# Seven-product matmuls in orders with more products between two uses of a bank

## The chip, the cores and the metric

The kernel runs on one core of a Trainium2 chip. A core has a matrix engine (TensorE, PE in the profile, with its weight loads shown apart as PEld), a vector engine (VectorE, DVE), a scalar engine (ScalarE, ACT), a general engine (GpSimd, POOL) and a synchronization engine (SyncE, SP), which here issues nearly all DMA transfers. Each engine runs its own instructions in order; semaphores make one wait for another. Matmul results go to PSUM, [...]from which ACT and DVE read them.

The metric is the device time of one execution, in microseconds, as the median of several runs. Lower is better.

## The reference

There are 16 independent batch items of 1024 nodes and 256 channels, and one 1024 x 1024 weighted adjacency matrix that they share. All is fp32. Cut to what matters, for each item:

```
# layer 0: attention whose queries come from a weighted graph product
A   = 2*| |sigmoid(diff of node means) - 0.5| - 0.5 |     # symmetrized
g   = relu((x^T @ (adj * A)) * para)                      # queries
k,v = x @ kv_w                                            # keys and values, 4 heads of 64
x   = layernorm(x + softmax(g k^T * scale) v)             # this is x1
# layer 1: two graph convolutions
h   = relu(x @ w1_loop + adj @ (x @ w1_neigh) + b1)       # 256 -> 128
h   = relu(h @ w2_loop + adj @ (h @ w2_neigh) + b2)       # 128 -> 256
x   = layernorm(x + (x + h) / 2)
```

## The kernel before

Items go through a software pipeline, one round per item. In round b the kernel computes the attention of item b, the first graph convolution of item b-1 together with the second of item b-2, the last normalization of item b-3, and the queries, keys and values of item b+1. The loop over b is written out by hand at line 1434; every engine gets its instructions in the order in which the Python code calls them, and nothing is reordered afterwards. Rounds 2 to 14 take the branch at line 1611 for the keys, values and queries, and rounds 2 to 15 compute the inner products below.

Most matrix products are made in the manner of Strassen and Winograd: a product of two-by-two blocks needs seven products instead of eight, of sums of blocks. The code numbers them 1 to 7. The seven are summed in pairs and chains: a PSUM bank gets product 1, is copied to SBUF, then product 6 is added onto it (the argument again=True), it is copied again, and so on. [...]each product that adds onto a bank waits until the copy of that bank has ended. Weights of a product are loaded by an instruction of their own (LDWEIGHTS), which carries the wait.

Three stages of a round concern us.

**Keys and values** (class KeysValues, line 420). Each key product is one call of key (two fp32 matmul records of 512 columns); each value product one call of value (four calls and eight records of 128 columns). start makes products 1 and 2 of both; middle makes 6, 5, 7 and 3, and end makes 4. Keys and values alternate. Products 1, 6, 5 and 3 use the bank k_first (v_first for values), 7 and 4 use k_next (v_next). Copies of banks are on ACT, final additions on DVE. The factors are sums of blocks: those of x are made by DVE (sums, line 430), those of the weights were made once, lie in DRAM as kv_sums and are fetched by load (line 448) in each round: 512 KB on SP's queue, right behind the two 512 KB transfers of para, which the scaling of the queries (line 693) reads. That scaling and the scaling of the normalization are called through later, between the sixth pair of products and the additions.

**Inner products** (fast_inner, line 961). x1 @ w1_neigh and x1 @ w1_loop are one seven-product scheme: with x1's channel-by-node blocks w11, w12, w21 and w22 and sums of them made by DVE in inner_sums (line 949). There are three banks, upper, lower and chain. Product 1 and then 6, 5 and 3 go to chain, 2 to upper, 7 and 4 to lower. The result t1T is transposed and stored to DRAM, to be fetched again by nodes; the other result, loops, holds x1 @ w1_loop until the convolution is done. fast_inner comes after the first half of the attention (both_units, line 785, called with pair 0) and is followed by the scores of the second half. both_units calls part_sum (a row sum for the softmax denominators) and then summed, which is inner_sums.

**The end of the graph convolutions** (Joined.run, line 1304, and last_products, line 1110). The convolution's seven products share their banks with the last products of item b-2. At the end DVE has these steps in order: the sum of u3, settle(1, 1) with it (line 1105: relu, then added to the residual), the addition of the loop terms, loop + first (line 1368), which frees the bank first, then rest, with the products 4 and 3 and their settle steps. The next products on PE, g_ps for the queries, begin in the bank first.

```
            rest = c2.last_products(third, second)
            self.product(3, first, again=True, steps=range(TJ // 2, TJ))
...
                loop = c1.loops[:, FB:N]
                nc.vector.tensor_add(loop, loop, first)
                c1.relu(1, loop)
            rest()
```

Of the kernel before, what the change touches and what calls it, by code (L numbers as in the profile page):

```python
# [18 lines left out]
def kernel(  # L19
# [31 lines left out]
    nc = tc.nc  # L51

    B, N, C = x.shape
# [6 lines left out]
    FB = 512  # L60
# [27 lines left out]
    def half_psum(name):  # L88
        return big_psum(name)[:, 0:FB]

    def bank_psum(name):
        return psum.tile([P, FB], F32, tag="bank", name=name, bufs=2)
# [327 lines left out]
    class KeysValues:  # L420
# [40 lines left out]
        def value(self, n, dst, again=False):  # L461
            for t in range(TJ):
                nc.tensor.matmul(dst[:, ts(t, P)], self.w[n][:, ts(t, P)], self.a[1][n],  # L463
                                 start=not again and t == 0, stop=True, skip_group_check=again or t > 0)

        def run(self, between=lambda: None, later=lambda: None, lowered=lambda: None):
            self.start()
            self.middle(between, later, lowered=lowered)
            return self.end()
# [23 lines left out]
        def block(self, i, j):  # L493
            return self.v[:, ts(j, TJ), ts(i, P)]

        def tiles(self, t):
            return t.rearrange("p (t c) -> p t c", c=P)
# [200 lines left out]
    class Attention:  # L698
# [86 lines left out]
        def both_units(self, pair, first=lambda: None, second=lambda: None, third=lambda: None, summed=None):  # L785
            u = NJ * pair
            self.scores(u, 0)
            self.scores(u + 1, NT, summed=False)
            row = row_tile(f"o_{self.b}_{pair}")
            self.collect(u + 1, 1)  # L790
            first()
            self.collect(u + 1, 2, 3)
            second()
            self.outputs(u, half_psum, turned=False)
            self.collect(u + 1, 4, 5)
            pav, self.o[u] = self.o[u], row
            nc.vector.transpose(row[:, 0:FB], pav)
            self.collect(u + 1, 6, 7)
            accB = self.turned_sum(u + 1)
            if summed:  # L800
                self.part_sum(u + 1, accB)
                summed()
            self.outputs(u + 1, turned=False)
            nc.vector.transpose(row[:, FB:N], self.o.pop(u + 1))
            if not summed:
                self.part_sum(u + 1, accB)
            third()
# [115 lines left out]
    class GraphConv:  # L923
# [25 lines left out]
        def inner_sums(self):  # L949
            w11, w12, w21, w22 = (self.xT[:, cc, ts(j, FB)] for cc in range(NC) for j in range(NJ))  # L950
            t13, t24 = (row_tile(f"X_{self.b}_{k}") for k in range(2))
            t1, t3, t2, t4 = t13[:, 0:FB], t13[:, FB:N], t24[:, 0:FB], t24[:, FB:N]
            nc.vector.tensor_sub(t1, w12, w11)
            nc.vector.tensor_sub(t2, w22, t1)
            nc.vector.tensor_sub(t3, w22, w12)
            nc.vector.tensor_sub(t4, w21, t2)
            s1, s2, s3, s4 = (self.w1[:, ts(n, P)] for n in range(4))
            self.inner_factors = {1: (w1n_sb[:, 0, :], w11), 2: (w1n_sb[:, 1, :], w21), 3: (s4, w22),
                                  4: (w1l_sb[:, 1, :], t4), 5: (s1, t1), 6: (s2, t2), 7: (s3, t3)}

        def fast_inner(self, aside=lambda: None):
            b = self.b

            def product(n, dst, again=False):
                w, xs = self.inner_factors[n]
                nc.tensor.matmul(dst, w, xs, start=not again, stop=True, skip_group_check=again)  # L966

            upper, lower, chain = (half_psum(f"in_ps_{b}_{i}") for i in range(3))
            s12, s34, t1T, self.loops, t1B = (row_tile(f"in_{b}_{i}") for i in range(5))
            p1, u2, u3, p7 = s12[:, 0:FB], s12[:, FB:N], s34[:, 0:FB], s34[:, FB:N]  # L970
            product(1, chain)
            nc.scalar.copy(p1, chain)
            product(2, upper)
            nc.vector.tensor_add(t1T[:, 0:FB], p1, upper)
            aside()
            product(6, chain, again=True)
            nc.scalar.copy(u2, chain)
            product(7, lower)
            nc.scalar.copy(p7, lower)
            product(5, chain, again=True)  # L980
            nc.scalar.copy(u3, chain)
            nc.vector.tensor_add(self.loops[:, FB:N], u3, p7)
            product(4, lower, again=True)
            nc.vector.tensor_add(self.loops[:, 0:FB], u2, lower)
            product(3, chain, again=True)
            nc.scalar.copy(t1T[:, FB:N], chain)
            nc.vector.transpose(t1B, t1T)
            self.t1d = dram.tile([N, HID], F32, tag="t1d", name=f"t1d_{b}", bufs=2)
            for a in range(Q):
                nc.sync.dma_start(out=self.t1d[:, a * S:(a + 1) * S].rearrange("(bn k) r -> k bn r", k=S),  # L990
                                  in_=by_node(t1B[a * S:(a + 1) * S, :]))
# [118 lines left out]
        def last_products(self, a, c):  # L1110
            name = f"h2_{self.b}"
            d = bank_psum(f"{name}_ps")
            snaps = [row_tile(f"{name}_{k}") for k in range(2)]
            p1, u2, u3 = snaps[0][:, 0:FB], snaps[0][:, FB:N], snaps[1][:, 0:FB]
            self.seventh_part(1, a)
            nc.scalar.copy(p1, a)
            self.seventh_part(2, d, start=True)
            nc.vector.tensor_add(p1, p1, d)
            self.settle(0, 0, p1)
            self.seventh_part(6, a)  # L1120
            nc.scalar.copy(u2, a)
            self.seventh_part(5, c)
            self.seventh_part(7, a)
            nc.scalar.copy(u3, a)
            nc.vector.tensor_add(u3, u3, c)
            self.settle(1, 1, u3)

            def rest():
                self.seventh_part(4, a)
                self.settle(1, 0, a)  # L1130
                self.seventh_part(3, c)
                nc.vector.tensor_add(u2, u2, c)
                self.settle(0, 1, u2)

            return rest
# [238 lines left out]
    def run():  # L1374
# [11 lines left out]
        q = Queries(0, x_first)  # L1386
        for t in range(NT):
            q.load(t)
        kv = KeysValues(0, xT)
# [5 lines left out]
        tiles = {mt: adj_blocked(mt) for mt in (0, TJ, 1)}  # L1395
# [34 lines left out]
        kT, v = kv.end()  # L1430
# [3 lines left out]
        for b in range(B):  # L1434
# [8 lines left out]
            if more:  # L1443
                q = (FastQueries if c1 else Queries)(b + 1, xb)
# [63 lines left out]
            elif more:  # L1508
# [10 lines left out]
                def summed():  # L1519
                    c1.inner_sums()  # L1520
                    if c3:
                        c3.deviation_aside()
# [88 lines left out]
            elif both and more:  # L1611
                q.pair(2)
                q.step(0)
                q.step(1, norm.mean, 5)
                q.pair(3)
                norm.squares()
                q.step(2)
                norm.sum_squares()
                q.load_para()
                kv.load()  # L1620
                q.step(3, lambda: norm.variance(bank_psum), 4)
                qT = q.end(kv.sums, lambda: None)
                xB = load_blocked(b + 1, f"a{b + 1}")
                load_next()
                kT, v = kv.run(later=lambda: (q.scale(), norm.scale()))
                norm.spread()
                att.watch()
            elif more:
                q.pair(2)
                q.step(0)  # L1630
                q.step(1, lambda: att.add(3), 5)
                q.pair(3)
                q.step(2, norm.mean)
                q.load_para()
                kv.load()
                q.step(3)
                qT = q.end(norm.sum_squares, norm.squares)
                xB = load_blocked(b + 1, f"a{b + 1}")
                load_next()
                first, second, third = adj_sum_steps(quarters, 3)  # L1640
                kT, v = kv.run(lambda: (first(), norm.variance()), q.scale, second)
                att.watch()
                third()
                norm.scale()
                norm.spread()
            else:
                c2.load_x()
                both.fetch("00", "10", 2, 3)
                c1.load_t1()
                both.left(nc.gpsimd)  # L1650
                both.fetch(1, 4, "11")
                both.run({1: (lambda: att.add_pairs(1), att.watch), 6: (norm.mean, norm.squares, norm.sum_squares),
                          5: (lambda: norm.variance(bank_psum),), 4: (norm.scale, norm.spread)}, last=nc.vector)
                c1.turn(0)
                c1.turn(1)
# [35 lines left out]
    with tc.If(count < P):  # L1691
        with tc.For_i(0, B, 1) as b:
            xb = load_x(b, "z")
            xT = channel_major(load_blocked(b, "z"), "xT_z")
            q = Queries("z", xb)
# [50 lines left out]
```

## Time and profile before

| What | Value |
|---|---|
| Time, median of 3 runs | 2123.66 us (2123.23 to 2124.41) |
| The profiled execution, its own time | 2123.94 us |
| Its span, first to last instruction | 2122.2 us, mean granted TensorE clock 0.999 |
| PE busy | 2106.6 us (99%), 8360 matmul records |
| DVE busy | 1884.2 us (89%) |
| ACT busy | 1251.8 us (59%) |
| POOL busy | 363.6 us (17%) |
| Inner products' matmuls (line 966) | 196 records in 14 stages |
| Key products (line 459) | 224 records |
| Value products (line 463) | 896 records |
| DMA queue of SP | 363.07 MB, 66.5% of the time of 16 engines |

How to read it: a line such as "943.13 1.98 PE L966 MATMUL in_ps<-x1T,w1n_sb 128*128 128x512 f32 x4" of the timeline gives the start, the duration of the merged instructions, the engine, the line of the kernel, the operation, what is written from what, the shapes and how many instructions are merged. In square brackets stand the idle time of the engine before it and what ended it. A row of the table of windows gives a stretch of time, its length, the busy time of each engine in it with the number of its instructions, the granted clock, the mean busy share of a DMA engine and the GB/s moved. Matmuls are pipelined, and the recorded end of one lies beyond the start of the next.

### The profile page before, as it was taken

The numbers are of one execution on the slowest core, as the hardware profiler recorded it, in microseconds if no ns is written. First come the engines' busy times: TensorE is split into PE (matmuls) and PEld (weight loads), VectorE is DVE, ScalarE is ACT, GpSimd is POOL, SyncE is SP. The second block draws the span as 40 slices with busy tenths as digits, with TensorE's granted clock in tenths as the row PEclk, the third lists the DMA queues.
The fourth block names the chain that finished last, engine by engine and source line by source line (L and its number), as shares of the span: only waits on it lengthen the run. The fifth ranks groups of instructions, "written<-read, shape, count | busy, mean of one in ns | idle before, by whom it ended". The sixth has DMA issues, their size and how long they took to land.

```text
span 2122.2 us, 24759 instructions
## 1 busy us (share of the span) xinstructions
PE 2106.6 (99%) x8360; PEld 996.1 (47%) x8360; DVE 1884.2 (89%) x2212; ACT 1251.8 (59%) x2126; POOL 363.6 (17%) x224
## 2 busy tenths in 40 slices
PE   9999999999999999999999999999999999999998
PEld 5344434445354453544535445354443534445355
DVE  6899998989989899898998989989899898989875
ACT  5845574556756566564765747557475584655523
POOL 2011103131021311213122031210312103131022
PEclk9999999999999999999999999999999999999999
DMA  8495756666648776476764768657596574966455
GB/s 216 122 175 186 150 149 199 124 224 138 185 154 156 244 127 195 151 146 237 139 204 149 139 226 164 208 131 158 195 174 215 134 161 173 184 214 130 140 187 179
DMA packets 688694, 364.98 MB, mean 172 GB/s; under 512 B 550705, under 2 KB 629937, under 8 KB 688561
## 3 DMA queue, kind: packets, MB, share of 16 engines
q1 hardware_dynamic: 688288, 363.07, 66.5%
q8 instruction: 68, 1.11, 0.2%
q14 instruction: 66, 0.53, 0.1%
q10 hardware_dynamic: 272, 0.26, 0.0%
HBM read 305.46 MB, written 57.80 MB: 171 GB/s over the span
## 4 chain that ended last, share of the span: by engine, by line
PE 94%; DVE 3%; DMA 2%; issue 0%; SPq 0%; ACT 0%; POOL 0%; POOLq 0%; DVEq 0%
PE s L726 21%; PE av L772 20%; PE hu_ps L1301 16%; PE g_ps L671 15%; PE v_ps L463 4%; PE k_ps L459 4%; PE in_ps L966 4%; PE hu_ps L1103 4%; PE g_ps L590 2%; DMA kv_sums<-kv_sums 2%; DVE acc L747 1%; PE h_ps L1014 1%; PE u_ps L1043 1%; PE h_ps L1103 1%; PE t_ps L940 0%
## 5 line engine op out<-in xcount | busy, mean ns | idle before, releaser
L747 DVE TENSOR_TENSOR acc<-acc,pr 128x1024 f32<-128x1024 f32 x384 | 481.1, 1253 | 34.3 <-ACT pr L731 0.9
L726 PE MATMUL s<-qT,kT 64*128 64x512 f32 x2048 | 448.9, 593 | 0.0
L772 PE MATMUL av<-pr,v 128*64 128x512 f32 x2048 | 447.0, 594 | 0.0
L733 ACT ACTIVATE pr<-s 128x1024 f32<-128x1024 f32 x392 | 390.9, 1116 | 41.3 <-PE s L726 41.2
L726 PEld LDWEIGHTS s<-qT,kT 64*128 64x128 f32 x2048 | 195.3, 187 | 241.3 <-issue 176.9
L772 PEld LDWEIGHTS av<-pr,v 128*64 128x64 f32 x2048 | 144.0, 137 | 297.3 <-issue 267.4
L1301 PE MATMUL hu_ps<-adj,R 128*128 128x512 f32 x480 | 213.6, 592 | 0.0
L376 POOL TENSOR_TENSOR rstd<-rstd,neg_half 128x32 f32<-128x32 f32 x16 | 88.4, 5522 | 566.7 <-DVE rstd L374 566.7
L582 DVE SCALAR_TENSOR_TENSOR wg<-wg,adj 128x1024 f32<-128x1024 f32 x128 | 168.9, 1358 | 3.6 <-ACT wg L577 3.6
L731 ACT ACTIVATE pr<-s 128x512 f32<-128x512 f32 x240 | 142.4, 702 | 0.0
L576 ACT ACTIVATE wg<-c_row,c_sums 128x1024 f32<-128x1024 f32 x120 | 139.4, 1162 | 2.7 <-DVE accB L754 1.0
L1301 PEld LDWEIGHTS hu_ps<-adj,R 128*128 128x128 f32 x480 | 90.0, 190 | 107.1 <-issue 98.8
L577 ACT ACTIVATE wg<-wg 128x1024 f32<-128x1024 f32 x128 | 135.4, 1057 | 4.1
L1301 PE MATMUL hu_ps<-adj,t 128*128 128x512 f32 x240 | 109.2, 598 | 0.0
L671 PE MATMUL g_ps<-wg,x 128*128 128x512 f32 x224 | 109.0, 599 | 0.0
L671 PE MATMUL g_ps<-T,xB 128*128 128x512 f32 x208 | 107.3, 597 | 0.0
L671 PE MATMUL g_ps<-wg,xB 128*128 128x512 f32 x208 | 106.2, 592 | 0.0
L1324 ACT COPY snap<-hu_ps 128x512 f32<-128x512 f32 x15 | 8.8, 586 | 157.5 <-PE hu_ps L1301 136.2
L1164 POOL TENSOR_TENSOR rstd<-rstd,neg_half 128x8 f32<-128x8 f32 x12 | 19.6, 1637 | 476.4 <-DVE rstd L1163 476.4
L745 DVE TENSOR_TENSOR acc<-pr,pr 128x1024 f32<-128x1024 f32 x64 | 77.9, 1217 | 21.5 <-ACT pr L733 21.5
L1292 POOL TENSOR_TENSOR R<-h 128x512 f32<-128x512 f32 x14 | 20.7, 1476 | 422.5 <-PE av L772 397.2
L754 DVE STREAM_TRANSPOSE accB<-acc 128x1024 f32<-128x1024 f32 x64 | 79.7, 1245 | 3.1
(289 smaller groups left out, 3297.7 us busy)
## 6 DMA issues: line engine op xcount, KB each, us to landing
adj<-adjT SPq DMA_DIRECT2D x210, 512.0 KB
adj<-in_adj_dram SPq DMA_DIRECT2D x128, 512.0 KB
para<-in_L_gnn_para_dram SPq DMA_DIRECT2D x32, 512.0 KB
xB_a<-in_x_dram SPq DMA_DIRECT2D x128, 128.0 KB
x1d<-xB_a SPq DMA_DIRECT2D x128, 128.0 KB
x<-x1d SPq DMA_DIRECT2D x16, 1024.0 KB
xB<-in_x_dram SPq DMA_DIRECT2D x120, 128.0 KB
x<-in_x_dram SPq DMA_DIRECT2D x15, 1024.0 KB
```

What stands on the lines that cost most here:

```text
L376: nc.gpsimd.tensor_tensor(self.rstd, self.rstd, neg_half, ALU.pow)
L576: nc.scalar.activation(wg, self.c_row, AF.Abs, bias=self.c_col[:, t:t + 1], scale=-1.0)
L577: nc.scalar.activation(wg, wg, AF.Tanh, scale=-0.5 / C)
L582: nc.vector.scalar_tensor_tensor(wg, wg, 1.0, self.adj.pop(t), op0=ALU.add, op1=ALU.mult)
L671: nc.tensor.matmul(self.p[n], x_n[:, k, :], w_n, start=(k == 0), stop=(k == TJ - 1))
L726: nc.tensor.matmul(halves[s], self.kT[rows, pair, ts(mt, P)], self.qT[rows, pair, ts(j, FB)], start=True, stop=True)
L731: nc.scalar.activation(pr[:, ts(s, FB)], halves[s], AF.Exp)
L733: nc.scalar.activation(pr, ps, AF.Exp)
L747: nc.vector.tensor_add(self.acc, self.acc, prs[mt])
L772: nc.tensor.matmul(pav[s * HD:(s + 1) * HD, :], self.v[:, mt, pair * P + s * HD:pair * P + (s + 1) * HD], prs[mt][:, ts(s, FB)], start=(mt ...
L1103: nc.tensor.matmul(dst[:, ts(t, P)], a[:, ts(t, P)], w, start=first, stop=True, skip_group_check=not first)
L1301: nc.tensor.matmul(dst, self.x[n][:, k, :], of_rows(rows, k), start=(start and k == 0), stop=(k == TJ - 1), skip_group_check=again)
```

## The change

There are five edits.

- run_spread is new, and takes the place of middle and end in rounds 2 to 14 only. The order of the products becomes 1, 2, 6, 7, 5, 4, 3, keys and values still alternating; later is called after the products 5. Banks and sums stay, so that three products stand between any two on one bank.
- kv.load is called ahead of q.load_para, which puts the transfer of kv_sums ahead of the two of para on SP's queue.
- fast_inner makes 1, 2, 7, 6, 3, 4, 5. Product 3 starts afresh in the bank upper instead of being added onto chain; t1T and loops now get chain by two additions on DVE, where before an ACT copy gave t1T and a DVE addition of two copies gave loops. There is one copy less on ACT and one addition more on DVE in each of the 14 stages.
- inner_sums comes ahead of part_sum in both_units, and makes t3 first.
- settle(1, 1, u3) is moved into rest, behind the addition of the loop terms.

```diff
--- before.py
+++ after.py
@@ -462,6 +462,37 @@
             for t in range(TJ):
                 nc.tensor.matmul(dst[:, ts(t, P)], self.w[n][:, ts(t, P)], self.a[1][n],
                                  start=not again and t == 0, stop=True, skip_group_check=again or t > 0)
+
+        def run_spread(self, later):
+            copy, add = nc.scalar.copy, nc.vector.tensor_add
+            kT, block, tiles = self.kT, self.block, self.tiles
+            (_, u1, u3, p7), (_, z1, z3, y7) = self.ksnap, self.vsnap
+            k_first, v_first = self.k_first, self.v_first
+            self.key(6, k_first, again=True)
+            copy(u1, k_first)
+            self.value(6, v_first, again=True)
+            copy(z1, v_first)
+            k_next, v_next = half_psum(f"k_ps_{self.b}_2"), bank_psum(f"v_ps_{self.b}_2")
+            self.key(7, k_next)
+            copy(p7, k_next)
+            self.value(7, v_next)
+            copy(y7, v_next)
+            self.key(5, k_first, again=True)
+            copy(u3, k_first)
+            self.value(5, v_first, again=True)
+            copy(z3, v_first)
+            later()
+            self.key(4, k_next, again=True)
+            add(kT[:, 1, FB:N], u3, p7)
+            add(kT[:, 1, 0:FB], u1, k_next)
+            self.value(4, v_next, again=True)
+            add(block(1, 1), tiles(z3), tiles(y7))
+            add(block(1, 0), tiles(z1), tiles(v_next))
+            self.key(3, k_first, again=True)
+            copy(kT[:, 0, FB:N], k_first)
+            self.value(3, v_first, again=True)
+            copy(block(0, 1), tiles(v_first))
+            return kT, self.v
 
         def run(self, between=lambda: None, later=lambda: None, lowered=lambda: None):
             self.start()
@@ -798,8 +829,8 @@
             self.collect(u + 1, 6, 7)
             accB = self.turned_sum(u + 1)
             if summed:
+                summed()
                 self.part_sum(u + 1, accB)
-                summed()
             self.outputs(u + 1, turned=False)
             nc.vector.transpose(row[:, FB:N], self.o.pop(u + 1))
             if not summed:
@@ -950,9 +981,9 @@
             w11, w12, w21, w22 = (self.xT[:, cc, ts(j, FB)] for cc in range(NC) for j in range(NJ))
             t13, t24 = (row_tile(f"X_{self.b}_{k}") for k in range(2))
             t1, t3, t2, t4 = t13[:, 0:FB], t13[:, FB:N], t24[:, 0:FB], t24[:, FB:N]
+            nc.vector.tensor_sub(t3, w22, w12)
             nc.vector.tensor_sub(t1, w12, w11)
             nc.vector.tensor_sub(t2, w22, t1)
-            nc.vector.tensor_sub(t3, w22, w12)
             nc.vector.tensor_sub(t4, w21, t2)
             s1, s2, s3, s4 = (self.w1[:, ts(n, P)] for n in range(4))
             self.inner_factors = {1: (w1n_sb[:, 0, :], w11), 2: (w1n_sb[:, 1, :], w21), 3: (s4, w22),
@@ -967,23 +998,23 @@
 
             upper, lower, chain = (half_psum(f"in_ps_{b}_{i}") for i in range(3))
             s12, s34, t1T, self.loops, t1B = (row_tile(f"in_{b}_{i}") for i in range(5))
-            p1, u2, u3, p7 = s12[:, 0:FB], s12[:, FB:N], s34[:, 0:FB], s34[:, FB:N]
+            p1, u2, p3, p7 = s12[:, 0:FB], s12[:, FB:N], s34[:, 0:FB], s34[:, FB:N]
             product(1, chain)
             nc.scalar.copy(p1, chain)
             product(2, upper)
             nc.vector.tensor_add(t1T[:, 0:FB], p1, upper)
             aside()
+            product(7, lower)
+            nc.scalar.copy(p7, lower)
             product(6, chain, again=True)
             nc.scalar.copy(u2, chain)
-            product(7, lower)
-            nc.scalar.copy(p7, lower)
-            product(5, chain, again=True)
-            nc.scalar.copy(u3, chain)
-            nc.vector.tensor_add(self.loops[:, FB:N], u3, p7)
+            product(3, upper)
+            nc.scalar.copy(p3, upper)
             product(4, lower, again=True)
             nc.vector.tensor_add(self.loops[:, 0:FB], u2, lower)
-            product(3, chain, again=True)
-            nc.scalar.copy(t1T[:, FB:N], chain)
+            product(5, chain, again=True)
+            nc.vector.tensor_add(t1T[:, FB:N], p3, chain)
+            nc.vector.tensor_add(self.loops[:, FB:N], p7, chain)
             nc.vector.transpose(t1B, t1T)
             self.t1d = dram.tile([N, HID], F32, tag="t1d", name=f"t1d_{b}", bufs=2)
             for a in range(Q):
@@ -1123,9 +1154,9 @@
             self.seventh_part(7, a)
             nc.scalar.copy(u3, a)
             nc.vector.tensor_add(u3, u3, c)
-            self.settle(1, 1, u3)
 
             def rest():
+                self.settle(1, 1, u3)
                 self.seventh_part(4, a)
                 self.settle(1, 0, a)
                 self.seventh_part(3, c)
@@ -1616,13 +1647,14 @@
                 norm.squares()
                 q.step(2)
                 norm.sum_squares()
+                kv.load()
                 q.load_para()
-                kv.load()
                 q.step(3, lambda: norm.variance(bank_psum), 4)
                 qT = q.end(kv.sums, lambda: None)
                 xB = load_blocked(b + 1, f"a{b + 1}")
                 load_next()
-                kT, v = kv.run(later=lambda: (q.scale(), norm.scale()))
+                kv.start()
+                kT, v = kv.run_spread(lambda: (q.scale(), norm.scale()))
                 norm.spread()
                 att.watch()
             elif more:
```

## The prediction

> **What bounds the kernel now.** First the page: busy times, then the chain that ended last.
>
> ```profile
> span 2122.2 us, 24759 instructions
> ...
> PE 2106.6 (99%) x8360; PEld 996.1 (47%) x8360; DVE 1884.2 (89%) x2212; ACT 1251.8 (59%) x2126; POOL 363.6 (17%) x224
> ...
> PE 94%; DVE 3%; DMA 2%; issue 0%; SPq 0%; ACT 0%; POOL 0%; POOLq 0%; DVEq 0%
> ```
>
> TensorE (PE) sets the end, VectorE (DVE) is second. So only PE time counts, and what can be won is pauses between products. "99% busy" hides those, since a matmul's recorded end lies beyond the start of the next; I measure from start to start. An fp32 product of 512 columns is two records 0.43 us apart, 0.86 us in all (640.99 to 641.85 in the timeline); a value product is eight of 0.11 us, 0.89 us.
>
> Second, the table of windows, each from the first key product to the first score. The thirteen stages that the change touches sum to 166.05 us. Two rows, then PE and SyncE (SP) in the longer one from the timeline:
>
> ```profile
> 640.99:654.71 13.72, 12.67 (x71) 8.93 (x70) 12.33 (x17) 7.50 (x12) 3.25 (x1) 1.00 0.99 194
> ...
> 1295.10:1307.53 12.43, 12.43 (x72) 8.85 (x70) 12.26 (x17) 7.50 (x12) 3.25 (x1) 1.00 1.21 214
> ```
> ```profile
> 635.77 1.51 SPq L566 DMA_DIRECT2D para<-in_L_gnn_para_dram  x2
> 637.38 0.38 SPq L451 DMA_DIRECT2D kv_sums<-kv_sums  x1
> ...
> 643.60 1.05 PE L463 MATMUL v_ps<-kvw_sb,xT 128*128 128x128 f32 x8
> 645.70 1.10 PE L459 MATMUL k_ps<-K,kv_sums 128*128 128x512 f32 x2 [1.05 <-DMA kv_sums<-kv_sums]
> ```
>
> The fifth product, due at 644.49, starts at 645.70: the weight sums landed late, 8.3 us after an issue that stood behind two parameter transfers. Seven of the thirteen stages take 12.50 or more; the excess is 166.05 - 13 x 12.43 = 4.4 us. The waits name the transfer for 2.7 of it, in three stages; in the others the same product is late by less, and DVE's sums that it also needs had ended (643.84 here, 0.65 before it was due), so I put it all there.
>
> Third, the inner products (window rows of 6.46 us in stages 2 to 13 of fourteen; the first 7.90, the last 6.52), with weight loads (PEld) and copies from the timeline:
>
> ```profile
> 944.29 0.59 ACT L972 COPY in<-in_ps 128x512 f32<-128x512 f32 x1 [5.77 <-PE in_ps L966]
> 944.93 0.30 PEld L966 LDWEIGHTS in_ps<-X,w_sums 128*128 128x128 f32 x2 [0.65 <-ACT in L972]
> 945.46 0.19 PEld L966 LDWEIGHTS in_ps<-X,w_sums 128*128 128x128 f32 x1 [0.24 <-issue]
> 945.92 0.65 DVE L974 TENSOR_TENSOR in<-in,in_ps 128x512 f32<-128x512 f32 x1
> 946.73 0.30 PEld L966 LDWEIGHTS in_ps<-X,w_sums 128*128 128x128 f32 x2 [0.65 <-ACT in L977]
> ```
>
> Products 6, 5 and 3 add onto the bank just copied. The copy ends 0.05 us before the load at 944.93, a load that otherwise comes 0.43 us ahead of its product (943.66, 944.09); the next record comes 0.53 us later and not 0.43-0.45. One late load costs about 0.08 us. 14 x 0.43 = 6.02; the other 0.44 is three late loads (0.25) and 0.1 at each change of tile shape (into and out of the stage).
>
> Fourth, the step from the graph convolution to the next queries:
>
> ```profile
> 1006.98 0.69 DVE L1107 SCALAR_TENSOR_TENSOR x<-h,x 128x512 f32<-128x512 f32 x1
> 1007.58 0.68 DVE L1368 TENSOR_TENSOR in<-in,hu_ps 128x512 f32<-128x512 f32 x1
> 1008.18 0.68 DVE L1107 SCALAR_TENSOR_TENSOR x<-hu_ps,x 128x512 f32<-128x512 f32 x1
> 1008.32 0.30 PEld L671 LDWEIGHTS g_ps<-wg,x 128*128 128x128 f32 x2 [0.19 <-DVE in L1368]
> ```
>
> The query product needs the bank that the loop terms' addition (L1368) reads. The last value-like product starts at 1007.26 and lasts 0.89, so it is due at 1008.15; it starts at 1008.32, and its load is late as well (0.10): 0.27 us, the same in all thirteen rounds.
>
> **What the Trainium skill says.** "TensorE: Matmul & The Clock Gate", section "Step-by-step: what each phase is for": weight loads, and they alone, are pulled ahead of running matmuls. The loads at 943.66 and 944.09 agree, and 944.93 is one that a wait held back. "PSUM — Partial Sum Buffer", section "PSUM bank collisions raise a hardware error": two engines may not be in one bank at once, so accesses are guarded by bank; hence the wait. "Perfetto Trace Analysis", section "Matmuls": rotate groups through banks so that their evacuation overlaps other matmuls, which is this change. "DMA: Bandwidth & Descriptors", section "Queues, rings and completion order": descriptors are consumed in ring order on each DMA engine, though completion isn't strictly so; the late third transfer agrees.
>
> **The change, part by part.**
>
> *Keys and values, 13 stages.* The transfer of the sums moves ahead of the parameters' two, nothing else on SP's queue moves: issued 1.6 us earlier (635.77 for 637.38). The longest lateness was 1.2, so all of it goes: -4.4 us. The reorder puts three products between two on one bank, where 6 and 5 had one; a copy (0.59, and 0.2 of drain: 641.85 to 642.05) always ends in time, and so do ScalarE's (ACT) ten copies at one per product, 0.59 against 0.87. In the 12.43 stages it removes 0.05 and 0.03 at the two products 5 (1300.35, 1301.26, 1302.18): 12.35 is 7 x 0.86 + 7 x 0.89 + 0.1 for the change of shape. -1.0 us. New waits: product 7 comes two places earlier, 5.25 us into the stage; its value bank is freed by DVE's addition L491, ending 5.28 + 0.68 = 5.96 in, against 6.11 for the value product: no loss, but only 0.15 spare. Product 3 is last but one; its bank is the first score's. Its copy stands on ACT behind two ReLUs (2.00 us; in the 902.71 stage from 912.40 to 914.40, which less that stage's lateness is 9.5 to 11.5 in) and runs 11.56 to 12.14; the score is due at 12.35. Hidden, 0.2 spare. Sum -5.4.
>
> *Inner products, 14 stages.* Order 1, 2, 7, 6, 3, 4, 5: two products between those on a bank. Removed: three late loads, 0.25. Added: product 3 now starts afresh on product 2's bank and must wait for DVE's addition L974. That ends at 946.57, 3.44 us into the stage, in every steady round; product 3 is due at 3.54. Its load is late by part: from 0 to 0.08, I take 0.05. Behind it wait 4, 5 and the scores. Twelve stages x -0.20 = -2.4. The last: L974 comes earlier, -0.3. The first: 7.90 because the subtractions came late (product 6 at 292.29). They now precede the 1.22 us row sum, but that sum then stands ahead of the addition, which ends near 294.6 instead of keeping product 3's 292.6: stage about 8.3, +0.4. Sum -2.3. Moving the row sum 2.6 us later costs nothing: its reader, the denominators, comes after the whole second score stage. One copy less on ACT (0.59) is off the path. DVE gets one addition more (0.65) before its transposition; it then waits 1.18 us for the first exponentials (idle before the 952.73 addition), which covers it; without that cover it would delay 14 x 0.65 = 9 us of additions. The bank of 5, 6 and 1 is freed by that addition 7.7 us in; the score that takes it is due at 8.9.
>
> *Loop terms.* L1368 changes places with the 0.60 us step ahead of it. Its product ended near 1006.53, so it runs 1006.98 to 1007.66, and the query product is no longer held: 13 x -0.27 = -3.5. The step put back still ends where L1368 ended, and the two later ones stay. In the round after them the transposes at 2052.70 wait on the same addition for 0.3, which goes too. Sum -3.8.
>
> Together -5.4 - 2.3 - 3.8 = -11.5 us. The profiled execution took 2123.94 us (span 2122.2 and 1.7 around it), 0.3 over the median 2123.66; taken from the median: 2112.2.
>
> **Rivals.** (A) The new waits eat the reorders: product 3's load late in full, and in each key stage a late first score and value product 7, 0.18 together. Then inner products give 1.9, key stages 5.4 - 13 x 0.18 = 3.1, loop terms 3.8: -8.8, 2115. For it: spares of 0.1 to 0.2; against: times that repeat to 0.01 us. (B) The parameters become the late transfer. Third in the row they land where the sums did, 4.7 us into the stage at worst; their multiply (L695) runs at 5.9 to 8.2. That leaves about 1.2 us; a landing 1.9 us later than that in all thirteen stages gives back 13 x 0.7 = 9: 2121, no difference. Against: nothing but their place in the row changes. (C) Slower: product 3 waits for L974 as a rule. DVE has no idle time ahead of it, and the addition stands behind an output transposition and the row sum. Each 1 us of lateness in 13 stages gives 13; from 1.2 us on (an end at 4.7 instead of 3.44) the kernel is slower by over 0.2%; at 1.5 it is 2112.2 + 19.5 = 2131.7. Against: the same instructions precede it as before. (D) That the order isn't carried out is excluded: the changed program has the new order on every engine.
>
> **How the numbers follow.** My sum 0.76, A 0.13, B 0.07, C 0.04. Faster 0.89 (sum and A), same 0.07, slower 0.04; 0.2%, 4.2 us, is about what a measurement can tell from no change. Low end: product 3 never late (0.6 more) and the first inner stage down to 6.2 (2.1 more), -14.2: 2109.5, and 1 us for the spread of the runs (2123.23 to 2124.41): 2108.5. High end between A and B: 2119.
>
> **What would show it.** Right: all thirteen key windows near 12.35, no PE wait on kv_sums; inner windows near 6.26; query products no longer waiting on the loop addition. Wrong: product 3 waiting on the addition that was L974 by more than 0.1, a first score waiting on the key copy, or the query scaling waiting on a DMA.

## The result and the profile after

The changed kernel takes 2112.69 us (median of 6 runs, 2111.48 to 2113.85), the kernel before 2123.64 in the same series (6 runs, 2120.74 to 2124.41). The ratio is 0.995, with a 95% interval of 0.9937 to 0.9963. The forecast was 2112.2. The profiled execution took 2112.32 us, its span is 2110.5; before they were 2123.94 and 2122.2.

The page of the kernel after, its span, TensorE and VectorE busy times and the chain that ended last by engine:

```profile
span 2110.5 us, 24762 instructions
...
PE 2096.5 (99%) x8360; PEld 996.7 (47%) x8360; DVE 1890.5 (90%) x2226; ACT 1247.0 (59%) x2112; POOL 364.4 (17%) x224
...
PE 97%; DVE 2%; DMA 0%; issue 0%; SPq 0%; ACT 0%; DVEq 0%; POOLq 0%
```

The share of PE in the busy list is 99% before and after and tells nothing. The chain tells it: the 2% that stood on DMA are gone, and one of the 3% on DVE. In code below line 465 the numbers are now 31 higher: the inner products stand at L997, the addition that frees product 2's bank at L1005, the settle step at L1138, the loop terms' addition at L1399.

The table of windows of the kernel after, two key and value stages and one stage of inner products (stretch and length, then the busy time of PE, PEld, DVE, ACT and POOL with counts, PE's clock, DMA share, GB/s):

```profile
639.31:651.67 12.36, 12.36 (x71) 8.80 (x69) 12.29 (x18) 7.18 (x11) 3.25 (x1) 1.00 1.13 201
1286.65:1299.01 12.36, 12.36 (x71) 8.80 (x70) 12.29 (x18) 7.18 (x11) 3.25 (x1) 1.00 1.32 207
938.43:944.67 6.24, 6.24 (x17) 2.50 (x15) 6.21 (x9) 2.35 (x4) 1.64 (x1) 1.00 0.02 4
```

The first is the stage that took 13.72 before. All thirteen take 12.36 now, 160.69 us in all, against 166.05. The inner stages take 8.36, then twelve times 6.24, then 6.21: 89.4 against 91.9. The timeline of the kernel after, around the key stage that starts at 639.31:

```profile
633.62 0.65 SPq L451 DMA_DIRECT2D kv_sums<-kv_sums  x1
634.31 1.34 SPq L597 DMA_DIRECT2D para<-in_L_gnn_para_dram  x2
...
642.81 1.02 PE L459 MATMUL k_ps<-K,kv_sums 128*128 128x512 f32 x2
643.67 1.05 PE L463 MATMUL v_ps<-kv_sums,K 128*128 128x128 f32 x8
...
650.89 0.59 ACT L492 COPY kT<-k_ps 128x512 f32<-128x512 f32 x1
...
651.67 0.70 PE L757 MATMUL s<-qT,kT 64*128 64x512 f32 x2
```

The first product that reads the sums starts 3.50 us into the stage with no idle time in brackets. The sums are issued 5.69 us ahead of the stage, where before it was 3.61 (637.38 against 640.99): 2.1 us earlier, though the reorder of the queue accounts for 1.6 only. The rest comes back below. The last key copy ends at 651.48, 0.19 us ahead of the score that it would have held. The same view of an inner stage:

```profile
941.19 0.65 DVE L1005 TENSOR_TENSOR in<-in,in_ps 128x512 f32<-128x512 f32 x1
...
941.89 0.30 PEld L997 LDWEIGHTS in_ps<-x1T,w_sums 128*128 128x128 f32 x2 [0.59 <-DVE in L1005]
941.97 1.05 PE L997 MATMUL in_ps<-x1T,w_sums 128*128 128x512 f32 x2
...
942.86 1.02 PE L997 MATMUL in_ps<-X,w1l_sb 128*128 128x512 f32 x2
```

Product 3 starts when due, at 938.43 + 3.54, though its load waited for VectorE's addition; the next product comes 0.89 us later and not 0.86, so the late load costs 0.03. And at the end of the graph convolution:

```profile
1001.93 0.68 DVE L1399 TENSOR_TENSOR in<-in,hu_ps 128x512 f32<-128x512 f32 x1
1002.53 0.68 DVE L1138 SCALAR_TENSOR_TENSOR x<-h,x 128x512 f32<-128x512 f32 x1
1002.65 0.72 ACT L1036 ACTIVATE h1T<-in,b_sb 128x512 f32<-128x512 f32 x1 [2.13 <-DVE in L1399]
1003.12 0.30 PEld L702 LDWEIGHTS g_ps<-wg,x 128*128 128x128 f32 x2
```

The query product's load has no wait left. The addition ends at 1002.61, half a microsecond ahead of it. ScalarE's ReLU of the loop terms (L1036) moves up with it.

From start to start, the parts sum as follows: keys and values -5.4; inner products -2.5; the convolution's end -2.1 (from the product hu_ps<-w2n_sb,uT, at 1000.05 before, to the first query product: 8.27 before and 8.11 now, 13 times); the second record of the query product, now 0.43 behind the first instead of 0.53, -1.3; the last round's transposes -0.3. Together -11.6, and the span lost 11.7. Differences outside these parts cancel: the first key product of the program starts 0.35 later, the one key stage ahead of the thirteen, which the change doesn't touch, takes 12.43 and not 12.82, the scores behind the first inner stage are 0.3 shorter, and the last 64 us are 0.4 longer. A round took 130.03 us before where nothing came late, and takes 129.47 now: 0.07 of keys, 0.22 of inner products and 0.27 at the convolution's end.

The list of PE's waits after, its first rows (total, times, longest):

```profile
PE in_ps L997 <- DVE in L1005: 1.9, 1, 1.9
PE idle L1415 <- POOL ident masks.py:199: 1.5, 1, 1.5
```

The one new wait of size is that of product 3 in the first inner stage. In the last round the second half of the transposes now waits 0.3 us, for another step; their start still comes 0.3 earlier than before.

### The profile page after: what moved, and what is told of

Same layout as the page of the kernel before. It is cut to its first block, busy times and chain, and to the rows that moved or that the text cites. A ratio compares the mean times of both kernels' runs of the same rounds, so it can differ in the third digit from the quotient of the medians.

```text
span 2110.5 us, 24762 instructions
## 1 busy us (share of the span) xinstructions
PE 2096.5 (99%) x8360; PEld 996.7 (47%) x8360; DVE 1890.5 (90%) x2226; ACT 1247.0 (59%) x2112; POOL 364.4 (17%) x224
## 4 chain that ended last, share of the span: by engine, by line
PE 97%; DVE 2%; DMA 0%; issue 0%; SPq 0%; ACT 0%; DVEq 0%; POOLq 0%
PE s L757 21%; PE av L803 20%; PE hu_ps L1332 17%; PE g_ps L702 16%; PE v_ps L463 5%; PE k_ps L459 5%; PE in_ps L997 4%; PE hu_ps L1134 4%; PE g_ps L621 3%; DVE acc L778 1%; PE h_ps L1045 1%; PE u_ps L1074 1%; PE h_ps L1134 1%; PE t_ps L971 0%; DMA x<-in_x_dram 0%
```

## Experiments

They were made in three groups; the kernel before took 2123.03 us in the first (e1 to e4), 2122.42 in the second (e5 to e8) and 2123.32 in the third (e9 to e12). My theory: each part of the change takes away its own pauses of PE, and they add. The first group does one part alone each.

**The transfer of the sums alone** (e1), on the kernel before.

```diff
                 norm.sum_squares()
+                kv.load()
                 q.load_para()
-                kv.load()
```

> The kernel before with one edit: the weight sums' transfer ahead of the parameters' two. My theory (the parts are separate pauses of TensorE, and what one of them gives is not taken back later): all thirteen key and value stages fall to 12.43 us, sum 161.6 for 166.05; time -4.4 us, about 2119.2, no TensorE wait on kv_sums. Rival (what is won is taken back at a later wait, because VectorE or a transfer is as late as TensorE): stages shorter, but the time hardly moves, less than 2 us. Second rival (the parameters become the late ones): the query scaling waits on a DMA and the stages don't get shorter.

Measured: 2119.51 us, ratio 0.9984 (0.9977 to 0.9991), -3.5. In its table of windows the stage that took 13.72 before:

```profile
641.24:653.68 12.44, 12.44 (x72) 8.86 (x70) 12.27 (x17) 7.50 (x12) 3.25 (x1) 1.00 1.30 210
```

All thirteen are alike, 161.64 us in sum, 4.4 less than before, and PE waits for kv_sums nowhere. The sums' place behind the parameters caused the lateness, and nothing waits for the parameters in their stead.

**The order of keys and values alone** (e2): run_spread called instead of run, the transfer left in its place.

```diff
-                kT, v = kv.run(later=lambda: (q.scale(), norm.scale()))
+                kv.start()
+                kT, v = kv.run_spread(lambda: (q.scale(), norm.scale()))
```

> The kernel before with the new order of keys and values alone, the transfer where it was. My theory: the stages that had no late transfer fall from 12.43 to 12.35-12.36, those with a late one keep their lateness of up to 1.3 us; sum 165.0, time -1 us, about 2122.6, within what the runs can tell. Rival (the order is what makes room, and the late transfer doesn't matter once it is there): all thirteen at 12.4, time -5 us. Second rival (first score and value product 7 wait): stages above 12.5 each, +2 us.

Measured: 2122.78 us, ratio 0.9998 (0.9989 to 1.0006). Stages without lateness take 12.36, but others up to 13.76, with a sum of 165.46: the reorder gives 0.07 a stage, which the late transfers can hide in the median. By itself this part can't be told from no change.

**The inner products alone** (e3): fast_inner and inner_sums as after, with its call ahead of the row sum, all else as before.

> The kernel before with the new order of the inner products and the moved subtractions alone. My theory: steady stages 6.24 for 6.46, the first 8.4 for 7.9, the last 6.2 for 6.5; -2.5 us, about 2121.1. Rival (VectorE's added addition delays the second half of the attention): stages as short, but the time -1 us or more than before, and the first additions of the exponentials start later than before against the scores.

Measured: 2120.48 us, ratio 0.9991 (0.9984 to 0.9998), -2.5. The stages are 8.37, 6.24 and 6.21, as in the full change.

**The settle step alone** (e4), on the kernel before.

```diff
-            self.settle(1, 1, u3)
 
             def rest():
+                self.settle(1, 1, u3)
```

> The kernel before with the loop terms' addition moved up alone. My theory: the query products start 0.17 us earlier against the last product and their second record 0.10 earlier, 13 times, and 0.3 in the round after: -3.8 us, about 2119.8. Rival (the second and third query products then wait for the steps that are behind the addition): the first starts earlier, the second later by as much, time unchanged.

Measured: 2117.43 us, ratio 0.9971 (0.9961 to 0.998): -5.6, 1.8 more than expected. The convolution's end is as forecast (8.10, with the second query record at 0.43), but the key stages sum to 161.90: in this trace their lateness is almost gone too, although the sums still stand third in the queue. The traced execution took 2115.39 and is the fastest of the ten, so a median one may keep more of it. One timeline of the kernel before, of ScalarE and SP between the loop terms and the key stage that starts at 1032.90, tells what the step pulls along:

```profile
1008.30 0.72 ACT L1005 ACTIVATE h1T<-in,b_sb 128x512 f32<-128x512 f32 x1 [2.86 <-DVE in L1368]
...
1017.44 4.03 ACT L1178 ACTIVATE x<-x,shift,rstd 128x256 f32<-128x256 f32 x8
...
1021.50 0.39 SPq L1180 DMA_DIRECT2D out_dram<-x  x1
...
1029.25 0.38 SPq L451 DMA_DIRECT2D kv_sums<-kv_sums  x1
```

And the same of e4, where the key stage starts at 1028.28:

```profile
1003.21 0.72 ACT L1005 ACTIVATE h1T<-in,b_sb 128x512 f32<-128x512 f32 x1 [2.14 <-DVE in L1368]
...
1012.36 4.03 ACT L1178 ACTIVATE x<-x,shift,rstd 128x256 f32<-128x256 f32 x8
...
1016.41 0.39 SPq L1180 DMA_DIRECT2D out_dram<-x  x1
...
1024.10 0.43 SPq L451 DMA_DIRECT2D kv_sums<-kv_sums  x1
```

The ReLU that waits for the loop terms' addition heads a run of ScalarE without a gap. At its end stands the scaled output, and SP's store of it (L1180) waits for that; the parameters and the sums are queued behind the store. From ReLU to store it is 13.20 us in both. But the ReLU ran 24.60 us ahead of the key stage before, and runs 25.07 ahead of it in e4. So the store leaves 11.87 us ahead of the key stage and not 11.40, and the sums 4.18 and not 3.65. The store's lead hardly varies over the twelve stages that have one: 11.40 or 11.41 in all of them before and in e1, 11.86 or 11.87 in all but one in e4. New theory: the settle step also moves SP's queue half a microsecond up, and two edits remove the same lateness.

**The same with the run of ScalarE put back** (e9): e4 and one copy of 0.6 us behind the ReLU, whose result nothing reads.

```diff
                 c1.relu(1, loop)
+                nc.scalar.copy(c1.loops[:, 0:FB], loop)
```

> The loop terms' addition moved up alone, as in the earlier run of it, and one ScalarE copy of 512 columns (0.59 us, result unused) put behind the ReLU that follows it. My new theory (moving the addition up also moved ScalarE's run of work, and so SyncE's queue, 0.6 us up; that took the lateness of the weight sums away): the transfers are issued about 3.7 us ahead of the stage again and not 4.2, key and value stages with late sums come back, sum 163 to 167 for 161.9; the query products still start on time; time about -3.5 us, 2119.5. Rival (that run had no late sums by chance): the sum stays below 162.5, time -5.5 us.

Measured: 2119.27 us (21 runs), ratio 0.9984 (0.9977 to 0.999), -4.05 where e4 had -5.6. The convolution's end keeps its gain. Timeline, with the key stage at 1029.65:

```profile
1004.58 0.72 ACT L1005 ACTIVATE h1T<-in,b_sb 128x512 f32<-128x512 f32 x1 [2.13 <-DVE in L1368]
1005.21 0.60 ACT L1370 COPY in<-in 128x512 f32<-128x512 f32 x1
...
1018.30 0.39 SPq L1180 DMA_DIRECT2D out_dram<-x  x1
...
1025.92 0.38 SPq L451 DMA_DIRECT2D kv_sums<-kv_sums  x1
```

The store leaves at -11.35 again and the sums at -3.73, and six stages are late again, by up to 0.48 us. The sum of the thirteen, 162.82, lies between the theory's 163 and the rival's 162.5, in an execution that is the third fastest of the 21 (2117.72). The time is near the forecast of 2119.5 and far from the rival's -5.5. Together with the store's lead this fits that what e4 gained beyond the PE pauses came through ScalarE and SP. The two runs were on different chips, though, each beside the kernel before, and their intervals just overlap (0.9961 to 0.998 and 0.9977 to 0.999).

**The transfer put back in the full change** (e12).

```diff
                 norm.sum_squares()
-                kv.load()
                 q.load_para()
+                kv.load()
```

> The changed kernel with the weight sums' transfer back behind the parameters'. New theory (two edits take away the same lateness, the order of the transfers and the loop terms' earlier addition): hardly any stage is late, sum 160.7 to 162, time +0 to +1.5 us against the changed kernel. Rival (the parts add): sum 165, +4.4 us, 2117.

Measured: 2113.69 us, ratio 0.9957 (0.9943 to 0.9971), 2.4 above the changed kernel on the same chip (e10, 2111.32; five runs each, whose ranges overlap a little). Eleven key stages take 12.36 or 12.35; the two others take 12.50 and

```profile
1286.09:1299.43 13.34, 12.59 (x72) 8.96 (x70) 13.27 (x19) 7.17 (x11) 3.25 (x1) 1.00 1.12 186
```

where PE is busy 12.59 of 13.34 us. The key stages sum to 161.76, 1.1 more than in e10. If the parts added, the sum would have been 165 and the time about 2117; all five runs lie below that (at most 2115.26), so that rival falls. The median lost more than I expected (0 to 1.5), about half of what the rival gave, and more than the traced stages show. The traced execution is the fastest of the five (2112.68). So the transfer's place still matters in the full change; one trace is one sample of how often a stage is late.

**The sums between the two parameters** (e7), in the full change. The argument of load_para, whose edit isn't shown, says which of the two transfers it issues.

```diff
-                kv.load()
-                q.load_para()
+                q.load_para(1)
+                kv.load()
+                q.load_para(2)
```

> The changed kernel with the weight sums' transfer between the parameters' two. My theory (the lateness before was the place in the row, about 0.7 us of issue and of moving per transfer): the sums come 0.7 later than in the changed kernel, so that of the former lateness of up to 1.29 at most 0.5 is left in two or three stages; sum of the thirteen 161 to 162 for 160.7, time +0 to +1.5 us. Rival (the sums must be first, any place behind a parameter transfer is late): sum 164 or more, time +3 us or more.

Measured: 2113.80 us, ratio 0.996 (0.9944 to 0.9975). All thirteen stages take 12.36 (sum 160.68), better than I thought; in eleven of them the sums are issued some 5.0 us ahead (in the first two, where the queue stands otherwise, 15.1 and 3.9). So 5.0 us sufficed in these eleven stages of this trace. But it is the fastest of the four executions (2111.82), and the median is 1.1 us above the changed kernel's 2112.69 of the first series, as the theory's range allows. That first place isn't needed is not shown.

**The row sum behind the addition** (e5, and again as e11 beside e10). This is aimed at the new wait in the first inner stage. There part_sum, the row sum, comes ahead of the addition that frees product 2's bank; now it is moved behind it.

```diff
                 summed()
-                self.part_sum(u + 1, accB)
+                self.late_sum = lambda: self.part_sum(u + 1, accB)
...
-                c1.fast_inner(turn_next)
+                c1.fast_inner(lambda: (att.late_sum(), turn_next()))
...
-                c1.fast_inner()
+                c1.fast_inner(att.late_sum)
```

> The changed kernel with the row sum of the second unit moved once more: behind the addition that frees product 2's bank. My theory (that addition is what product 3 waits for, and only VectorE's queue makes it late): product 3 is on time in every stage, steady stages 6.21 for 6.24, the first 6.2 for 8.36; -2.5 us against the changed kernel, about 2110. Rival (the first stage is late because the attention before it is, and TensorE would wait for the next thing): first stage above 7.5, time within 1 us of the changed kernel.

> The changed kernel again, for a comparison on the same chip with the runs beside it: about -11 us against the kernel before, 2112.5.

> The changed kernel with the row sum behind the addition, again, beside the changed kernel itself. By the stage widths of its first trace (first inner stage 7.24 for 8.36, twelve of 6.21 for 6.24) it should be 1.5 us faster, 2111; if the difference of the first comparison (2.8) stands, something outside these stages gains too.

Measured: e5 2109.87 us, ratio 0.9941 (0.9928 to 0.9955). On one chip e10, the changed kernel once more, took 2111.32 (2110.97 to 2113.01) and e11 2109.92 (2109.80 to 2110.02): 1.4 us less, with ranges apart. The stages are 7.23 and then 6.21 in e11. The timeline of its first:

```profile
291.80 0.71 DVE L835 STREAM_TRANSPOSE o<-av 128x512 f32<-128x512 f32 x1
292.43 0.65 DVE L1005 TENSOR_TENSOR in<-in,in_ps 128x512 f32<-128x512 f32 x1
293.00 1.20 DVE L791 TENSOR_REDUCE den_part<-accB 128x32 f32<-128x1024 f32 x1
...
293.13 0.30 PEld L997 LDWEIGHTS in_ps<-x1T,w_sums 128*128 128x128 f32 x2 [1.56 <-DVE in L1005]
```

The addition ends 4.41 us into the stage, where the changed kernel has it at 5.54 (294.50 less 288.96), and product 3 is still 0.9 us late there. In the other stages its load no longer waits, which is the 0.03. The expected 6.2 for the first stage didn't come: ahead of the addition DVE still has the subtractions and an output transposition, without a gap. This is the fastest version found.

**The order of the subtractions and the row sum undone** (e8): the inner products of the change with inner_sums behind part_sum and t3 third, as before.

> The changed kernel with the row sum and the subtractions in their old order. My theory: product 7 needs its subtraction at 1.82 us into the stage and the old order has it ready at 1.57, and the addition product 3 waits for has the same work ahead of it either way: steady stages 6.24-6.26, the first 8.3, time unchanged within 1 us of the changed kernel. Rival (the moved subtractions carry the gain of the inner products): steady stages 6.4 or more, +2.5 us.

Measured: 2112.69 us, ratio 0.9954 (0.9939 to 0.997); stages 8.39, 6.25 and 6.21. In the first stage it is product 6 that pauses, 1.9 us, and in the changed kernel it is product 3, 1.9 us as well, both behind the same DVE work; first e8, then the changed kernel:

```profile
292.80 1.96 PE L997 MATMUL in_ps<-X,w_sums 128*128 128x512 f32 x4 [1.88 <-issue]
...
294.55 1.13 PE L997 MATMUL in_ps<-x1T,w_sums 128*128 128x512 f32 x2 [1.86 <-DVE in L1005]
```

The edit as made gives nothing; in e5 and e11, with the row sum behind the addition too, the stage is 1.1 us shorter.

**The addition late** (e6), for the rival in which product 3 waits. Two more additions of 512 columns are put ahead of it on DVE; their results are overwritten unread.

```diff
             product(2, upper)
+            t5 = self.inner_factors[5][1]
+            nc.vector.tensor_add(t1B[:, 0:FB], t5, t5)
+            nc.vector.tensor_add(t1B[:, 0:FB], t5, t5)
             nc.vector.tensor_add(t1T[:, 0:FB], p1, upper)
```

> The changed kernel with two additions of 512 columns (0.6 us each, results unused) put ahead of that addition on VectorE. My theory of product 3's wait: the addition ends 1.2 us later, and from a spare of 0.1 on every us is a us of TensorE: steady stages 7.35 for 6.24, first 9.6, last 6.8; +15 us against the changed kernel, about 2127.5, slower than the kernel before. Rival (VectorE gets its time back from TensorE's pause, or product 3 isn't bound to it): stages longer by less than 0.4, time +5 us at most.

Measured: 2131.27 us, ratio 1.0039 (1.0024 to 1.0055): slower than the kernel before. The addition ends 4.73 us into a steady stage and not 3.41, and the stage takes 7.56 and not 6.24; product 3 in it:

```profile
951.25 1.12 PE L997 MATMUL in_ps<-x1T,w_sums 128*128 128x512 f32 x2 [1.09 <-DVE in L1008]
```

Both grow by 1.32: once product 3 waits, DVE's time counts in full. The slope that the rival assumed is right, and what keeps the changed kernel on the good side of it is that the addition ends 0.13 us ahead of product 3's start. The first stage took 11.04, 1.4 more than the 9.6 expected. The table of windows, from product 3's start to the scores, tells why (the last figures are PE's clock, DMA share and GB/s):

```profile
295.66:296.62 0.96, 0.96 (x3) 0.48 (x3) 0.96 (x1) 0.00 (x0) 0.00 (x0) 1.00 0.00 0
296.62:297.93 1.31, 1.31 (x3) 0.53 (x2) 1.26 (x2) 0.59 (x1) 0.00 (x0) 0.65 0.00 0
297.93:299.78 1.85, 1.85 (x4) 0.34 (x2) 0.69 (x1) 0.00 (x0) 0.00 (x0) 0.50 0.01 4
```

Products 4 and 5 run at a clock of 0.65 and 0.50 and take 1.31 and 1.85 us (the second with the change of shape) instead of 0.86 and 0.95: 1.35 us, which is the miss.

## Why the prediction was right, and where it was not

*Keys and values: right in size.* -5.4 was forecast and -5.4 came; 12.36 a stage where 12.35 was worked out. The late transfer was worth 4.4 in the stages of e1, as forecast, and 3.5 by its median. The two spares that I named held: the value product 7 didn't wait, and the last key copy ended 0.19 ahead of the score.

*Inner products: right.* 6.24 for 6.26, the first 8.36 for 8.3, the last 6.21. Product 3's load was late by part, as taken: 0.03 was paid of a possible 0.08, not 0.05. That DVE's additional addition is covered held too: no score waits for the bank, which comes free at 946.13, 7.70 into the stage.

*Loop terms: right on PE, incomplete beyond it.* 13 x 0.27 and the 0.3 of the last round all came. The sentence "The step put back still ends where L1368 ended, and the two later ones stay" holds: it ends 0.87 us after the start of the last value-like product (1002.34), where L1368 ended 1.00 after it (1007.26). What failed is, in the part on keys and values, "nothing else on SP's queue moves", and the unspoken assumption that nothing follows the addition: the output store at the head of the queue leaves 11.85 us ahead of the key stage and not 11.41. I traced who waits for the step that was moved back, but not who waits for the addition that was moved up. Its ReLU heads an ACT run at whose end the SP queue waits, so this edit also brings the sums' transfer 0.5 us forward. Alone it gave -5.6 for the -3.8 of its term.

*The sum: right, for a reason that the prediction didn't see.* It charged the whole lateness (-4.4) to the transfer's place in the queue. Alone that is worth -3.5 in the medians; with the rest of the change in place, +2.4 when undone. The loop terms' edit removes a part of the same lateness: 1.8 of its -5.6 lies beyond its term, 1.55 was lost with ScalarE's run put back (e9), and 1.1 is the difference of 3.5 and 2.4. I counted the lateness once, so the total is right although its division among the edits is not unique. The four parts alone sum to -11.9 (-3.5, -0.3, -2.5, -5.6), or to -10.4 with e9's -4.05 for the last; the whole gave -11.0 in one series and -12.0 in another. So an overlap of 1.1 to 1.8 us, to which e4, e9 and e12 point, is hardly seen in the sum; the runs of the kernel before alone spread over 5.8 us (2120.35 to 2126.18 in the first group).

*The rivals.* A, the new waits eat the reorders: no; 0.03 a stage was paid of it. B, the parameters become the late transfer: no; neither PE nor DVE waits for them, in the change or in e1. C, slower: didn't come, and e6 shows that its mechanism and slope are real. *The low end* counted on the first inner stage falling to 6.2 and product 3 never late; e11 does the second in all stages but the first and half of the first point, and lands at 2109.9.

What stays open: why the same transfer, issued equally early, lands in time in one stage and 1.2 us late in another of the same execution (before: issued 3.61 us ahead of the stage at 640.99, which took 13.72, and 3.53 ahead of the one at 1815.27, which took 12.44). The trace shows what stands around it on SP's queue: ahead, the output store, four stores of h1d and the parameters; behind, loads of the next item. Which of them holds it up in one stage and not in another was not tested.

## What to carry to other kernels

For every step that moves, follow both directions: what waits for the step that goes back, and what the step that goes forward releases, through the other engines to the DMA queue at the end of the run. A transfer that is late by a varying amount can be helped at either end, by its place in the queue or by what lets the queue start; undo each edit within the full change before saying what it was worth. Where a product starts a fresh bank to avoid one wait, find the reader that frees that bank and put work that nobody hurries for, here a row sum, behind it.

## What was not expected of the hardware

After a pause of PE of 3.2 us (e6) the matrix engine's granted clock fell to 0.50, though the products had started again at 295.66 and the first of them still ran at 1.00:

```profile
295.66 1.12 PE L997 MATMUL in_ps<-x1T,w_sums 128*128 128x512 f32 x2 [3.19 <-DVE in L1008]
...
300.20:301.00 0.80, 0.80 (x4) 0.27 (x4) 0.80 (x2) 0.00 (x0) 0.00 (x0) 0.86 0.00 0
```

The 0.65 of the second row of e6's table puts the fall at 297.0; the 0.86 of the row here puts its end near 300.4: some 3.4 us. The Trainium skill, "TensorE: Matmul & The Clock Gate", section "What's actually happening", has an activity window of 3.4 us that runs freely, and half the clock after an idle one. The halved clock and the length of the slow stretch agree with it; the recorded pause here was 3.19, a little under 3.4, and was enough. The pauses of 1.9 us in the same stage of the changed kernel and of 1.1 in e6's steady stages brought no such fall. It is one occurrence, and no run here finds the limit.

A late weight load cost between 0.03 and 0.10 us here: 0.03 a product when it is held until 0.08 ahead of the product (the changed kernel), and 0.10 where it is held to the product's own start (the query product before).
